# Pairs of experts' tiles in an attention and mixture-of-experts kernel: earlier gathers and transposes, another order on VectorE, other buffers

## The chip, the cores and the metric

The kernel runs on one core of one Trainium2 chip. The metric is the device time of one execution in microseconds (us); lower is better. Five engines share the work: TensorE (PE in the profile, its weight loads PEld), VectorE (DVE), ScalarE (ACT), GpSimd (POOL) and SyncE (SP), which here only issues DMAs.

## What is computed

The input is 2 x 2048 tokens of 512 features. It is normalized to xn. One branch is attention with a single head of 512 over xn, causal, with a residual; the other a mixture of eight experts, of which each token takes two. The result is x + s * silu(ffn).

```python
xn = _layernorm(x)
s = attention(xn)            # layernorm again, q, k, v, causal softmax, o_proj, + xn
scores = xf @ gate_w.T + gate_b + bias
top_scores, top_idx = top_k(scores, 2)
gates = softmax(top_scores)
comb = sum(one_hot(top_idx, 8) * gates[..., None], axis=1)
h = silu(einsum('td,ehd->teh', xf, w1) + b1)       # 512 -> 352, for each expert
y = einsum('teh,edh->ted', h, w2) + b2             # 352 -> 512
ffn = einsum('ted,te->td', y, comb)
return x + s * silu(ffn)
```

## The kernel before

Everything is f32. The whole program stands in one order written out by hand (`manual_schedule`): each engine and each DMA queue takes its instructions in the order of the Python code, and a late one holds all behind it on the same engine.

**Projections and routing.** Tokens come in 8 blocks of 512. For each block the rows are normalized, transposed and multiplied by folded weights to q and v; the results go to memory in HBM. Blocks 0 to 4 use a scheme of seven half-size products instead of eight (`seven_products`, L395), whose additions VectorE makes into tiles `so` of a ring of four (L403), stored from ScalarE's queue. A normalized row also goes, as its two 16-bit halves, to `zu_d`, from which the experts' rows are gathered later. `route` (L455) is a generator: each `yield n` lets the loop at its call emit n projection units (each 8 matmul instructions) before it goes on. It picks two experts per token, counts, gives each (token, expert) a slot, and inverts that by one-hot matmuls (`inv_p`) into `toki`, the token of each slot. Then it gathers the first `FIRST` tiles of rows, and from `half` and `first` finds the expert of every half tile (`eidi`) and its bias column (`b1sel`, L674 to L702).

**Experts.** There are 68 tiles of 128 slots. Tiles 6 to 57 in the order of work are 26 pairs of one expert each (`paired`); six single tiles go ahead of them and ten after. A tile i passes through these steps, each a function:

- `gather(i)` (L799): GpSimd fetches its rows `xs` from `zu_d` by an indirect DMA;
- `turn(i)` (L868): SP transposes the 16-bit halves by DMA to `xhT`; `join(i)` (L873): VectorE puts the halves together to `xT`;
- `up(i)` (L907) on TensorE, or `up_pair(i)` (L952) with seven products for two tiles; the pairs take weight differences `w1s` made by `w1_sums` (L927) and row sums made by `x_sums` (L940), and VectorE adds the products to `h` (L975);
- `turn_h(i)` (L992): ScalarE scales h, GpSimd splits it to `hu` (L996), SP transposes it to `huT`; `join_h(i)` (L1003): VectorE joins it, ScalarE applies SiLU;
- `down(i)` (L1016) on TensorE, three tiles behind; `keep_y(i)` (L1031): the result goes through `y` to `y_d`.

`experts_step(i)` (L1038) orders this for a single tile, `pair_step(i)` (L1063) for a pair. Steps -5 to -1 (L1212) only fill the pipeline between the last projection units. Steps 0 to 5 are single tiles; after steps 1 to 4 `w1_sums` makes the four differences of two experts each, the third of each four on GpSimd (L938).

**Memory.** Buffers come from pools on a stack at either end of SBUF. A pool opened with `reuse_waits="tile"` waits tile by tile for what lay there before; the others wait for the whole of each earlier pool that they overlap. The pool `xtp`, with the tiles `xhT` and `xT`, is opened after routing's pools `rp` and `hot` are closed and lies where they lay. `wsp`, with `w1s`, is opened once the projections' pools are closed.

**Attention** follows, in steps of one or two tiles of queries, with seven products where it can (`values_first`, `values_next`, `values_end`, `combine_p`). `gate(s)` takes two gathered rows of y for each token to the gate, and the last pair's output is made ahead (`make_ahead`).

Of the kernel before, what the change touches and what calls it, by code (L numbers as in the profile page):

```python
# [13 lines left out]
U16 = mybir.dt.uint16  # L14
# [12 lines left out]
def gated_attention_moe(  # L27
# [166 lines left out]
    def load_w1(e):  # L194
        if e == 0:

            w1p = wp.enter_context(tc.tile_pool(name="w1p", bufs=1, reuse_waits="tile"))
            w1.append(w1p.tile([P, E, ND, H], F32, name="w1"))
        nc.sync.dma_start(
            out=w1[0][:, e, :, :], in_=w1_t[e].rearrange("(c p) h -> p c h", p=P)  # L200
        )
# [193 lines left out]
    def seven_products(b, of_q):  # L395
# [7 lines left out]
        outs = [fp.tile([P, 2, D], F32, name=f"so_{tag}_{i}", tag="so", bufs=4) for i in range(2)]  # L403
# [51 lines left out]
    def route():  # L455

        with ExitStack() as rt:
# [170 lines left out]
            for k, oh in enumerate((oh1, oh2)):  # L628
# [11 lines left out]
                for t0 in range(0, NT, GROUP):  # L640
# [19 lines left out]
                    yield 1  # L660
# [13 lines left out]
            GS = [P, E, NJ]  # L674
            ge = rp.tile(GS, F32, name="ge")
            begun = []
            for k in range(3):
                nc.vector.tensor_tensor(
                    ge, half.unsqueeze(1).to_broadcast(GS), first[:, k].to_broadcast(GS), ALU.is_ge
                )  # L680
                n = rp.tile([P, NJ], F32, name=f"begun{k}")
                over_e(n, ge, ALU.add)
# [7 lines left out]
            for e in range(E):  # L690
                nc.vector.tensor_scalar(ge[:, e, :], eid, float(e), None, ALU.is_equal)
            for c in range(NH):
                for e in range(E):
                    if e == 0:
                        nc.vector.tensor_scalar(
                            b1sel[:, c, :], ge[:, e, :], b1s[:, c, e : e + 1], None, ALU.mult
                        )
                    else:
                        nc.vector.scalar_tensor_tensor(
                            b1sel[:, c, :], ge[:, e, :], b1s[:, c, e : e + 1], b1sel[:, c, :],  # L700
                            ALU.mult, ALU.add,
                        )  # L702
# [52 lines left out]
    fold_st.close()  # L755
    both(0)
# [38 lines left out]
    xsp = st.enter_context(tc.tile_pool(name="xsp", bufs=6))  # L795
    xss = {}
    FIRST = 5
# [57 lines left out]
    xtp = st.enter_context(tc.tile_pool(name="xtp", bufs=1))  # L855
    hp = st.enter_context(tc.tile_pool(name="hp", bufs=3))
    yp = st.enter_context(tc.tile_pool(name="yp", bufs=3))
# [10 lines left out]
    def turn(i):  # L868
        xh = xtp.tile([P, 2 * ND, P], U16, name=f"xhT_{i}", tag="xhT", bufs=3)
# [3 lines left out]
    def join(i):  # L873
        xT = xtp.tile([P, ND, P], F32, name=f"xT_{i}", tag="xT", bufs=4)
# [52 lines left out]
    def w1_sums(e, parts):  # L927
# [6 lines left out]
        t = [w1s[0][:, e : e + 2, i] for i in range(4)]  # L934
        for i, x1, x2 in (1, b12, b11), (2, b22, t[0]), (3, b22, b12), (4, b21, t[1]):
            if i in parts:
                engine = nc.gpsimd if i == 3 else nc.vector
                engine.tensor_tensor(t[i - 1], x1, x2, ALU.subtract)  # L938
# [13 lines left out]
    def up_pair(i, meanwhile):  # L952
# [3 lines left out]
        hs = [hp.tile([P, H], F32, name=f"h_{i + k}", tag="h", bufs=4) for k in range(2)]  # L956
# [21 lines left out]
        meanwhile()  # L978
# [3 lines left out]
        add(c21, made(s3, t(3)), c12)  # L982
        p5 = made(s1, t(1))
# [8 lines left out]
    def turn_h(i):  # L992
        h = phs[i] if i in paired else hp.tile([P, H], F32, name=f"h_{i}", tag="h", bufs=4)
# [43 lines left out]

    def experts_step(i):  # L1038
# [8 lines left out]
        at(keep_y, -DOWN - 1)  # L1047
        if i >= 0:
            at(gather, FIRST)
        at(turn, 3)  # L1050
        if i + 1 not in xts:
            at(join, 1)
        if i < FULL:
# [9 lines left out]
    def pair_step(i):  # L1063
# [3 lines left out]
        turn(i + 3)  # L1067
        turn(i + 4)
        up_pair(i, lambda: join_h(i - 2))
        turn_h(i)  # L1070
        gather(i + FIRST + 1)
        turn_h(i + 1)
# [4 lines left out]
        for k in range(i + 2, i + 4):  # L1077
            join(k)
        if i + 2 in paired:
            x_sums(i + 2)  # L1080

# [134 lines left out]
    stage_a.close()  # L1216
    sm = right(att, name="sm2", bufs=4)
# [11 lines left out]
    for i in range(NS):  # L1229
# [17 lines left out]
        if i < paired.start:  # L1247
            if 0 < i <= E // 2:
                w1_sums(2 * (i - 1), (1, 2, 3, 4))
# [311 lines left out]
    for s in range(NT + OUT + 2):  # L1561
# [103 lines left out]
        elif fast and s == NT - 1:  # L1665
# [4 lines left out]
                + [lambda: combine_p(s - 1), lambda: gate(s - 1)],  # L1670
# [62 lines left out]
```

## Time and profile before

| | us |
|---|---|
| median of 3 runs (1054.21 to 1056.05) | 1054.82 |
| the profiled execution, in all | 1049.76 |
| its span, first to last instruction | 1048.1 |

| stage | from, us | to, us |
|---|---|---|
| projections and routing | 0 | 262.4 |
| six single tiles of the experts | 262.4 | 291.8 |
| 26 pairs | 291.8 | 540.4 |
| ten single tiles | 540.4 | 592.0 |
| attention | 592.0 | 1048.1 |

The stages are read off TensorE's timeline. The page groups instructions by source line, engine, operation and tiles; a row gives count, busy time, mean duration, and the idle time of the engine just before them with what ended it. The costliest rows of the parts concerned:

```profile
L996 POOL COPY hu<-h 128x704 uint16<-128x704 uint16 x68 | 63.7, 937 | 175.1 <-issue 129.6
...
L875 DVE COPY xT<-xhT 128x1024 uint16<-128x1024 uint16 x68 | 61.8, 916 | 25.2 <-DMA xhT<-xs 25.0
...
L975 DVE TENSOR_TENSOR h<-p,h 128x176 f32<-128x176 f32 x182 | 56.1, 337 | 15.2 <-PE p L968 8.0
L1005 DVE COPY ht<-huT 128x768 uint16<-128x768 uint16 x68 | 40.3, 592 | 33.2 <-DMA huT<-hu 31.4
```

### The profile page before, as it was taken

What the parts mean: (1) busy time and instruction counts of PE and PEld (TensorE: products, weight loads), DVE (VectorE), ACT (ScalarE), POOL (GpSimd) and SP (SyncE); (2) the same over time, 40 slices, a digit from 0 to 9 for tenths busy, and PEclk for the clock granted to TensorE, in tenths of its full rate; (3) what the DMA queues carried; (4) which work ended last, traced back from release to release, by engine and by line L of the source; (5) the groups of instructions that cost most, each with busy time, mean ns of one, the idle gap of its engine ahead of it and who ended that gap; (6) DMA issues with size and microseconds to landing.
All of it is one profiled execution on the core that took longest, in us unless ns stands there. A gap on an engine that the chain in (4) does not pass through costs nothing.

```text
span 1048.1 us, 13294 instructions
## 1 busy us (share of the span) xinstructions
PE 1027.8 (98%) x3836; PEld 643.9 (61%) x3836; DVE 735.2 (70%) x1449; ACT 367.2 (35%) x741; POOL 461.7 (44%) x474
## 2 busy tenths in 40 slices
PE   9998999999899999999999999999999999999997
PEld 5686887444466666677654346776764544447576
DVE  5796884796787767777754558786556556788667
ACT  3212122121244444444445423222334553542341
POOL 3363141002654434434433317444656777764272
PEclk9998999999999999999999999999999999999999
DMA  8699989964799999999999857535767868754361
GB/s 303 183 266 281 251 257 317 354 209 125 171 197 218 201 223 197 203 226 208 199 229 244 198 191 173 134 90 133 191 172 235 257 185 224 196 143 116 95 158 41
DMA packets 300519, 209.41 MB, mean 200 GB/s; under 512 B 234520, under 2 KB 247576, under 8 KB 299424
## 3 DMA queue, kind: packets, MB, share of 16 engines
q1 hardware_dynamic: 280960, 145.60, 59.1%
q0 software_dynamic: 10560, 35.17, 13.0%
q10 hardware_dynamic: 8928, 27.79, 7.4%
q8 instruction: 33, 0.54, 0.2%
q14 instruction: 38, 0.31, 0.1%
HBM read 92.89 MB, written 60.03 MB: 146 GB/s over the span
## 4 chain that ended last, share of the span: by engine, by line
PE 73%; issue 8%; POOL 7%; DMA 7%; DVE 4%; SPq 1%; ACT 0%; POOLq 0%; DVEq 0%
PE ps L1122 13%; PE py L1025 9%; PE p L1174 8%; PE p L1382 8%; PE p L412 8%; PE po L1334 7%; PE p L968 7%; PE pj L353 3%; PE pw L219 3%; PE pj L358 3%; PE p L1334 2%; POOL xs L801 2%; DMA huT<-hu 2%; POOL hu L996 1%; DMA zuT<-zu 1%
## 5 line engine op out<-in xcount | busy, mean ns | idle before, releaser
L1025 PE MATMUL py<-w,ht 128*128 (+3 forms) x408 | 182.2, 593 | 0.0
L1122 PE MATMUL ps<-k,q 128*128 128x512 f32 (+3 forms) x416 | 143.0, 495 | 0.8 <-DMA q<-qt_d 0.8
L996 POOL COPY hu<-h 128x704 uint16<-128x704 uint16 x68 | 63.7, 937 | 175.1 <-issue 129.6
L1294 POOL COPY pu<-pT 128x1024 uint16<-128x1024 uint16 (+2 forms) x74 | 82.3, 1143 | 117.9 <-ACT pT L1284 58.1
L1025 PEld LDWEIGHTS py<-w,ht 128*128 128x128 f32 (+3 forms) x408 | 73.4, 184 | 83.6 <-issue 76.4
L1122 PEld LDWEIGHTS ps<-k,q 128*128 128x128 f32 x416 | 74.7, 190 | 68.4 <-issue 59.5
L801 POOL DMA_INDIRECT xs<-zu_d,toki x68 | 75.1, 1105 | 69.5 <-DVE toki L669 57.8
L1011 ACT ACTIVATE ht<-ht,b1sel 128x128 f32<-128x128 f32 (+3 forms) x228 | 71.1, 378 | 79.8 <-DVE ht L1005 79.5
L1479 POOL DMA_INDIRECT yg<-y_d,posi x64 | 68.3, 1067 | 38.1 <-DVE yg L1490 22.6
L1334 PE MATMUL po<-v,pT 128*128 128x512 f32 x182 | 81.1, 592 | 0.0
L875 DVE COPY xT<-xhT 128x1024 uint16<-128x1024 uint16 x68 | 61.8, 916 | 25.2 <-DMA xhT<-xs 25.0
L276 POOL COPY zu<-z 128x1024 uint16<-128x1024 uint16 x32 | 35.2, 1100 | 83.2 <-DVE z L261 83.2
L975 DVE TENSOR_TENSOR h<-p,h 128x176 f32<-128x176 f32 x182 | 56.1, 337 | 15.2 <-PE p L968 8.0
L1005 DVE COPY ht<-huT 128x768 uint16<-128x768 uint16 x68 | 40.3, 592 | 33.2 <-DMA huT<-hu 31.4
L1316 DVE COPY pT<-puT 128x1024 uint16<-128x1024 uint16 (+2 forms) x74 | 55.3, 777 | 9.6 <-DMA puT<-pu 9.5
L425 DVE TENSOR_TENSOR so<-p,so 128x512 f32<-128x512 f32 x70 | 46.0, 685 | 18.3 <-DMA v_d<-so 8.2
L1334 PEld LDWEIGHTS po<-v,pT 128*128 128x128 f32 x182 | 34.2, 190 | 38.1 <-issue 36.4
L1284 ACT ACTIVATE pT<-pT,nm 128x1024 f32<-128x1024 f32 x14 | 16.1, 1148 | 111.4 <-DVE nm L1210 72.3
L1500 DVE SCALAR_TENSOR_TENSOR o<-xo,xscale,o 128x512 f32<-128x512 f32 x30 | 28.8, 967 | 33.2 <-ACT o L1497 31.0
L1180 DVE TENSOR_TENSOR pT<-p,pT 128x512 f32<-128x512 f32 x49 | 32.9, 687 | 25.9 <-PE p L1174 18.7
L1284 ACT ACTIVATE pT<-ps,nm 128x512 f32<-128x512 f32 (+3 forms) x52 | 30.0, 581 | 59.4 <-DVE nm L1210 38.9
L1508 POOL TENSOR_TENSOR o<-o,yg 128x512 f32<-128x512 f32 x30 | 41.4, 1381 | 14.9 <-DVE o L1500 14.7
(276 smaller groups left out, 2046.1 us busy)
## 6 DMA issues: line engine op xcount, KB each, us to landing
y_d<-y SPq DMA_DIRECT2D x68, 256.0 KB
zu_d<-zu SPq DMA_DIRECT2D x32, 264.0 KB
kt_d<-kT ACTq DMA_DIRECT2D x8, 1024.0 KB
k<-kt_d SPq DMA_DIRECT2D x32, 256.0 KB
q<-qt_d SPq DMA_DIRECT2D x32, 256.0 KB
v<-v_d SPq DMA_DIRECT2D x32, 256.0 KB
xo<-in_x_dram SPq DMA_DIRECT2D x32, 256.0 KB
x<-in_x_dram SPq DMA_DIRECT2D x30, 256.0 KB
```

The lines of the kernel that those rows point to most:

```text
L412: nc.tensor.matmul(ps[:, r, :], lhsT=lhs[:, c, ts(r, P)], rhs=rhs[:, c, :], start=(c == 0), stop=(c == 1),)
L801: nc.gpsimd.indirect_dma_start(out=xs, out_offset=None, in_=zu_d, in_offset=bass.IndirectOffsetOnAxis(ap=toki[:, order[i] : order[i] + 1], ...
L968: nc.tensor.matmul(ps, lhsT=x[:, c], rhs=y(c).rearrange("p o h -> p (o h)"), start=(c == 0), stop=(c == ND // 2 - 1),)
L996: nc.gpsimd.tensor_copy(hu[:, :, :H], h.bitcast(U16).rearrange("p (d h) -> p h d", h=2))
L1011: nc.scalar.activation(ht[:hn, c, at], ht[:hn, c, at], AF.Silu, bias=b1sel[:hn, c, j : j + 1])
L1025: nc.tensor.matmul(py[at, :], lhsT=ht[:k, c, at], rhs=rhs[n], start=(c == 0), stop=(c == NH - 1),)
L1122: nc.tensor.matmul(ps[:, :w], lhsT=aqs[seq[s] // 2][:, c, ts(t % 2, P)], rhs=aks[first + j][:, c, :w], start=(c == 0), stop=(c == ND - 1),)
L1174: nc.tensor.matmul(ps, lhsT=x[:, c], rhs=y[:, c], start=(c == 0), stop=(c == ND // 2 - 1))
L1294: nc.gpsimd.tensor_copy(pu[:, : 2 * w].rearrange("p (h d) -> p h d", h=2), turned[s][:, k : k + w].bitcast(U16).rearrange("p (d h) -> p h ...
L1334: nc.tensor.matmul(dst, lhsT=turned[s][:, ts(k, P)], rhs=avs[first + k // BT][:, k % BT, cols], start=(start and k == k0), stop=(k == k1 - 1),
L1382: nc.tensor.matmul(dst, lhsT=a[:, k], rhs=v(k), start=(k == 0), stop=(stop and k == n - 1))
L1479: nc.gpsimd.indirect_dma_start(out=y, out_offset=None, in_=y_d, in_offset=bass.IndirectOffsetOnAxis(ap=posi[k][:, n : n + 1], axis=0),)
```

## The change

1. `route`: the yield before the last group's inversion is left out. The comparisons are laid out with experts innermost, summed by `sum_e`; the eight comparisons and 24 scalings for `b1sel` become one comparison and three multiplications with a reduction.
2. A pool `xhp` with four `xhT` tiles is opened beside `xsp`, before `route`; `xsp` has seven tiles, `FIRST` is 6, and `turn` runs four tiles ahead instead of three.
3. `w1_sums(e, i)` makes one difference; three are made in each of steps 0 to 5 until all 16 are done, ahead of `join_h` and `up`; one of them is on GpSimd.
4. `pair_step`: the joins come first; `join_h(i - 2)` (`meanwhile`) comes after three additions; both `turn_h` come before the second gather.
5. `y` has two buffers instead of three, from a pool opened after the projections' pools are closed; `h` has three instead of four. `keep_y` of tiles 0 and 1 is on ScalarE.
6. The `so` tiles of v of blocks 0 to 3 have a pool `sop` of four tiles of their own.
7. Near the end of attention, `gate` comes between the first two and the last two operations of `combine_p`.

```diff
     def load_w1(e):
         if e == 0:
-
+            half_st.close()
...
-        outs = [fp.tile([P, 2, D], F32, name=f"so_{tag}_{i}", tag="so", bufs=4) for i in range(2)]
+        pool = fp if of_q or b == SEVEN - 1 else sop
+        outs = [pool.tile([P, 2, D], F32, name=f"so_{tag}_{i}", tag="so", bufs=4) for i in range(2)]
...
-                    yield 1
+                    if k == 0 or t0 + GROUP < NT:
+                        yield 1
                     invert()
...
-            GS = [P, E, NJ]
+            GS = [P, NJ, E]
             ge = rp.tile(GS, F32, name="ge")
+
+            def sum_e(dst):
+                nc.vector.tensor_reduce(dst, ge, AX.X, ALU.add)
+
             begun = []
             for k in range(3):
                 nc.vector.tensor_tensor(
-                    ge, half.unsqueeze(1).to_broadcast(GS), first[:, k].to_broadcast(GS), ALU.is_ge
+                    ge, half.unsqueeze(2).to_broadcast(GS),
+                    first[:, k, :, 0].unsqueeze(1).to_broadcast(GS), ALU.is_ge,
                 )
                 n = rp.tile([P, NJ], F32, name=f"begun{k}")
-                over_e(n, ge, ALU.add)
+                sum_e(n)
...
-            for e in range(E):
-                nc.vector.tensor_scalar(ge[:, e, :], eid, float(e), None, ALU.is_equal)
+            nc.vector.tensor_scalar(eid, eid, -1.0, float(E), ALU.mult, ALU.add)
+            mine_e = rp.tile(GS, F32, name="mine_e")
+            nc.vector.tensor_tensor(
+                mine_e, eid.unsqueeze(2).to_broadcast(GS),
+                rank[:, :, 0].unsqueeze(1).to_broadcast(GS), ALU.is_equal,
+            )
             for c in range(NH):
-                for e in range(E):
...
+                nc.vector.tensor_tensor(
+                    ge, mine_e, b1s[:, c, :].unsqueeze(1).to_broadcast(GS), ALU.mult
+                )
+                sum_e(b1sel[:, c, :])
...
+    half_st = ExitStack()
+    sop = half_st.enter_context(tc.tile_pool(name="sop", bufs=4, reuse_waits="tile"))
...
-    xsp = st.enter_context(tc.tile_pool(name="xsp", bufs=6))
+    xsp = st.enter_context(tc.tile_pool(name="xsp", bufs=7))
+    xhp = st.enter_context(tc.tile_pool(name="xhp", bufs=4))
     xss = {}
-    FIRST = 5
+    FIRST = 6
...
-    yp = st.enter_context(tc.tile_pool(name="yp", bufs=3))
...
     def turn(i):
-        xh = xtp.tile([P, 2 * ND, P], U16, name=f"xhT_{i}", tag="xhT", bufs=3)
+        xh = xhp.tile([P, 2 * ND, P], U16, name=f"xhT_{i}", tag="xhT")
...
-        for i, x1, x2 in (1, b12, b11), (2, b22, t[0]), (3, b22, b12), (4, b21, t[1]):
-            if i in parts:
-                engine = nc.gpsimd if i == 3 else nc.vector
-                engine.tensor_tensor(t[i - 1], x1, x2, ALU.subtract)
+        x1, x2 = ((b12, b11), (b22, t[0]), (b22, b12), (b21, t[1]))[i]
+        engine = nc.gpsimd if (e, i) == (0, 2) else nc.vector
+        engine.tensor_tensor(t[i], x1, x2, ALU.subtract)
...
-        hs = [hp.tile([P, H], F32, name=f"h_{i + k}", tag="h", bufs=4) for k in range(2)]
+        hs = [hp.tile([P, H], F32, name=f"h_{i + k}", tag="h") for k in range(2)]
...
         nc.scalar.copy(c11, made(a11, b(0, 0)))
-        meanwhile()
         p2 = made(a12, b(1, 0))
         add(c12, made(s2, t(2)), c11)
         add(c11, p2, c11)
         add(c21, made(s3, t(3)), c12)
+        meanwhile()
         p5 = made(s1, t(1))
...
+    sums_left = [(e, k) for e in range(0, E, 2) for k in range(4)]
...
-        at(keep_y, -DOWN - 1)
+        if 0 <= i - DOWN - 1 < NS:
+            keep_y(i - DOWN - 1, *[nc.scalar.copy] * (i < paired.start))
         if i >= 0:
             at(gather, FIRST)
-        at(turn, 3)
+        at(turn, 4)
         if i + 1 not in xts:
             at(join, 1)
+        for _ in range(3 if 0 <= i < paired.start else 0):
+            if sums_left:
+                w1_sums(*sums_left.pop(0))
...
         gather(i + FIRST)
-        turn(i + 3)
-        turn(i + 4)
+        for k in range(2):
+            turn(i + 4 + k)
+        for k in range(2):
+            join(i + 2 + k)
         up_pair(i, lambda: join_h(i - 2))
-        turn_h(i)
+        for k in range(2):
+            turn_h(i + k)
         gather(i + FIRST + 1)
-        turn_h(i + 1)
         join_h(i - 1)
         down(i - DOWN)
         keep_y(i - DOWN, nc.scalar.copy)
         down(i - DOWN + 1)
-        for k in range(i + 2, i + 4):
-            join(k)
...
     stage_a.close()
+    yp = st.enter_context(tc.tile_pool(name="yp", bufs=2))
...
-            if 0 < i <= E // 2:
-                w1_sums(2 * (i - 1), (1, 2, 3, 4))
...
-                + [lambda: combine_p(s - 1), lambda: gate(s - 1)],
+                + [lambda: combine_p(s - 1, (1, 3)), lambda: gate(s - 1)]
+                + [lambda: combine_p(s - 1, (2, 4))],
```

## The prediction

> **What bounds the kernel now.** I read the page first, then busy time by stretch, then TensorE's timeline where a stretch shows idle time, then who ended those waits.
>
> The page, row of busy time:
>
> ```profile
> PE 1027.8 (98%) x3836; PEld 643.9 (61%) x3836; DVE 735.2 (70%) x1449; ACT 367.2 (35%) x741; POOL 461.7 (44%) x474
> ```
>
> TensorE sets the time, and only its gaps can be won. "Busy" hides part of them (an instruction's modelled end runs into the gap), so I count from start to start. Busy time by stretch (us, PE, PEld, DVE, ACT, POOL, clock, DMA, GB/s):
>
> ```profile
> 262.40:293.10 30.70, 25.91 (x75) 14.31 (x74) 23.41 (x27) 8.11 (x19) 20.29 (x17) 0.94 0.77 170
> ...
> 340.10:446.60 106.50, 104.31 (x441) 70.97 (x440) 76.95 (x168) 48.34 (x121) 44.10 (x45) 1.00 1.07 206
> 446.60:540.40 93.80, 93.60 (x401) 64.51 (x400) 69.02 (x149) 44.48 (x110) 41.42 (x41) 1.00 1.04 215
> ```
>
> The start of the experts (six single tiles, before the pairs) is the worst stretch, and the only one of these whose clock is below 1.00. TensorE there:
>
> ```profile
> 262.01 0.59 PE L358 MATMUL pj<-wvo,kT 128*128 128x512 f32 x1
> 264.67 11.40 PE L915 MATMUL ph<-w,xT 128*128 x32 [2.06 <-issue]
> ...
> 280.49 2.63 PE L915 MATMUL ph<-w,xT 128*128 x8 [1.85 <-DVE xT L875]
> ...
> 294.21 0.83 PE L968 MATMUL p<-w1s,xs 128*128 x4 [0.96 <-DVE xs L949]
> ```
>
> and all engines around the first gap:
>
> ```profile
> 256.47 2.30 DVE L699 SCALAR_TENSOR_TENSOR b1sel<-ge,b1s,b1sel 128x76 f32<-128x76 f32 x7
> ...
> 258.99 6.77 SPq L870 DMA_TRANSPOSE xhT<-xs  x4
> ...
> 263.77 1.37 DVE L875 COPY xT<-xhT 128x1024 uint16<-128x1024 uint16 x2 [5.00 <-DMA xhT<-xs]
> ```
>
> The rows were gathered from 243.08 on, but SP issues the first transposes only when routing's last sum ends (258.77): their tile lies in routing's freed buffers. The later gaps follow GpSimd; the chain of waits:
>
> ```profile
> 288.89 2.30 POOL w1s L938
> ...
> 294.72 4.58 DMA huT<-hu
> ```
>
> The chain has such a subtraction in each of four steps. Each stands ahead of the next copy `hu`, hence of the transpose `huT`, `join_h`, and behind it, in VectorE's order, the next tiles' work. In the pairs VectorE's order matters; TensorE, then VectorE, in one bad step:
>
> ```profile
> 389.30 0.86 PE L968 MATMUL p<-w1s,xs 128*128 x4 [0.51 <-DVE xs L949]
> ...
> 392.51 0.86 PE L968 MATMUL p<-w1s,xT 128*128 x4 [0.56 <-DVE h L975]
> ```
> ```profile
> 385.35 0.89 DVE L1005 COPY ht<-huT 128x768 uint16<-128x768 uint16 x1 [2.54 <-DMA huT<-hu]
> ...
> 391.65 0.56 DVE L1005 COPY ht<-huT 128x768 uint16<-128x768 uint16 x1 [1.95 <-DMA huT<-hu]
> ```
>
> A late `huT` holds VectorE, and behind it the two joins and the sums `xs` that TensorE's third product needs, then the additions that free PSUM.
>
> [...] Here 98% busy goes with the gaps above. [...] the clock of the first stretch is 0.94, a loss of 0.06 x 30.7 = 1.8 us; but one gap of 2.06 us came before it, and the 1.85 us gap at 280.49 was not followed by slow matmuls. [...] Here one xT copy took 0.69 us at 265.90 and 2.15 us at 278.28 beside GpSimd's subtraction.
>
> **The change part by part.** The sum is made against the profiled execution (span 1048.1, 1049.8 in all); the runs' median of 1054.8 lies 5.0 above that, which I carry over unchanged.
>
> *Start, TensorE's own work.* An up takes 2.36 us and a down 2.58 (540.45 to 542.81 to 545.39, unhindered). Up to the first pair it has 6 ups and 3 downs: 14.2 + 7.7 = 21.9. The last projection ends issuing at 262.01 + 0.43 = 262.44. An undisturbed pair step takes 9.33 (312.11 to 321.44), the second starts at 302.43, so the first one's effective start is 293.10. 30.7 - 21.9 = 8.8 us are lost, 1.8 of them to the clock.
>
> *Start, what the edits leave.* The last inversion no longer waits behind a projection unit: its operands were ready at 237.33 and it ran at 241.32 after a unit of 3.43, so token indices and all six gathers come about 3.5 sooner. The last sums: three comparisons of 0.79 and three strided reductions of 1.18 now reduce along the innermost axis; VectorE's 1024-wide reduction at 1.21 gives about 0.75 for 608, my estimate. Then 8 x 0.12 + 3 x 0.25 + 21 x 0.33 = 8.6 become one compare and three times multiply and reduce, 0.8 + 3 x 1.55 = 5.4, plus 0.2 for one more scalar operation. They end near 250.8 instead of 258.8. The transpose tile now has a home that routing doesn't use, so SP starts it when gathers land (4.4 us), near 245, and xT0 and xT1 are joined before 255. That clears TensorE's first gap, except for a PSUM bank that ScalarE may still be reading (its copy ends at 263.23): 0.5 us left. The half clock should go with it.
>
> The 16 weight subtractions: three a step, in steps 0 to 5, now ahead of `join_h` and `up`, one alone on GpSimd. VectorE then runs 15 x 0.9 = 13.5, six or seven joins x 0.7 = 4.9, four join_h x 0.56 = 2.2, x_sums 1.7: 22.3 us. It cannot begin the subtractions before 262.6 (their tile overlays the projections' operands), so it ends near 285, while TensorE, freed, wants the first pair at 262.9 + 21.9 = 284.8. They run side by side with next to no slack; hu0 at 266.8, huT0 4.2 later and join_h near 272 put the first down some 0.5 late, and I allow 0.5 more. If the subtractions' tile also waited for the last projections' stores (near 266.5), the stage would lose 3.9 more; by the sizes of the tiles it doesn't reach them, so I take 0. Left: 1.5 of 8.8, gain 7.3 (3.4 to 8.3).
>
> *Pairs.* From 302.43 to 540.45 lie 25 steps: 238.0 - 25 x 9.33 = 4.7 lost. Now each transpose is issued a tile sooner, with a fourth buffer; the two joins (1.4 to 1.9) stand at the head of the step, where their transposes are a whole step old; `join_h(i-2)` comes after three additions, not before all seven. So sums `xs` follow `join_h(i-1)` directly, 1.4 us sooner, against shortages of 0.3 to 0.8, and the bank that the seventh product needs is freed ahead of `join_h`. VectorE has 7 x 0.34 + 2 x 0.92 + 2 x 0.59 + 2.07 = 7.5 of 9.33 us. The second gather now follows both `hu` copies, 1.2 us sooner for `huT`, later for a row that has a step to spare. I leave 1.0 lost: gain 3.7 (0 to 4.7).
>
> *Rings.* y falls from 3 to 2, h from 4 to 3. h: the copy that frees the slot ran a step before, nothing. y: stores are issued up to 3.5 us after the copy (309.73 to 313.24), landing took 4.93 in the chain (565.95), and the slot is wanted 9.33 after the copy: 0.9 us to spare. Queued behind a late ScalarE copy are the pair's first eviction and `join_h`'s SiLUs. Not below nothing, since a smaller ring speeds nothing; up to 0.5 x 26 = 13 against; I take 0.
>
> *sop.* Values' outputs leave the shared ring. At 86.38 VectorE waits 3.3 for a store, but then waits 2.6 more for the last `zuT`, which releases TensorE at 92.27; the transposes are held by full DMA queues. I take 0 (-0.5 to +3).
>
> *End.* Gating now fills VectorE while the last two sums wait; it stood 0.8 us for ScalarE at 1027.88, and the bank that TensorE misses at 1033.78 (gap 1.67) is freed behind that. Gain 0.8 (0 to 0.9). Copying y of two tiles on ScalarE: under 1.4 us of VectorE, within the start's margin.
>
> Sum: 7.3 + 3.7 + 0 + 0 + 0.8 = 11.8. Profiled span about 1036.3; median 1054.8 - 11.8 = **1043.0**.
>
> **Rivals.** *B, pairs' stalls stay*: DMA share 1.07 says that the transposes are late because DMA is full; against it, 446.6 to 540.4 lost 0.2 us of idle at 1.04. Gain 7.3 + 0.8: 1046.7. *C, VectorE bounds the start*: 22.3 us in 22 leaves nothing for GpSimd's interference (0.69 to 2.15 for one copy); 4 us back, and a part of the pairs': gain 4.5, 1050.3. *D, the y ring (slower)*: if stores land more than 0.9 us later than 4.93 in every pair, at 0.5 a step 13 us are lost and 11.8 won: 1056.0; it outweighs the gain from 0.45 us a step. For it: DMA is full; against: only the worst delays reach the bound. *E, nothing*: the gaps are refilled by others, 1054.8.
>
> **How the numbers follow.** A 0.60, B 0.18, C 0.10, D 0.08, E 0.04. A's own range is 1040 to 1046; with B and the near part of C the range is 1039.5 to 1049.5. Faster by over 0.2% (2.1 us, about what can be told from no change): A, B, C = 0.88; same 0.04; slower 0.08.
>
> **What would show it.** SP's first transposes near 245 and no gap before `up`; no half-clock stretch near 265; GpSimd with one `w1s`; first pair near 285; pair steps of 9.33 without the waits on `xs` and `h`; a gap of some 0.9 near the end. Wrong if ScalarE's y copies wait for DMA, if VectorE has no idle time from 263 to 285 and TensorE waits on it, or if the pairs' losses remain.

## The result, and the profile after

| | before | changed |
|---|---|---|
| median, us | 1054.51 (1050.91 to 1056.05, 4 runs) | 1039.58 (1037.34 to 1043.04, 4 runs) |
| profiled execution, in all | 1049.76 | 1043.04 |
| its span | 1048.1 | 1041.3 |

The ratio of the changed kernel to the one before is 0.9866, 95% interval 0.9828 to 0.9905: faster. The predicted 1043.0 is 3.4 us above the measured median. The medians lie 14.9 us apart, the two profiles only 6.7: the kernel before was profiled 4.8 us below its median, the changed one in the slowest of its four runs.

The ratios here and below use each kernel's runs within 1.5% of its fastest, which cuts off the upper part of the wide spread of the kernel before (1042.4 to 1086.5 in 59 runs of one series); a median set beside a median differs from the ratio for that reason, and both are given where they disagree.

The page, row of busy time:

```profile
PE 1023.0 (98%) x3836; PEld 643.8 (62%) x3836; DVE 727.0 (70%) x1426; ACT 366.7 (35%) x743; POOL 463.4 (45%) x471
```

Busy time by stretch (us, PE, PEld, DVE, ACT, POOL, clock, DMA, GB/s): the six single tiles up to the effective start of the first pair, then pairs.

```profile
259.28:292.16 32.88, 26.45 (x91) 15.87 (x89) 24.46 (x30) 10.28 (x24) 19.33 (x16) 0.99 0.88 171
300.00:530.00 230.00, 230.00 (x993) 159.86 (x992) 165.37 (x368) 106.58 (x270) 101.98 (x97) 1.00 1.01 213
```

In the pairs TensorE is busy all of the time. The start has not become shorter: 32.9 us against 30.7. TensorE there:

```profile
259.28 7.26 PE L923 MATMUL ph<-w,xT 128*128 x24
268.36 2.63 PE L923 MATMUL ph<-w,xT 128*128 x8 [1.82 <-DVE xT L883]
271.67 2.84 PE L1032 MATMUL py<-w,ht 128*128 x6 [0.68 <-ACT ht L1018]
...
286.63 0.83 PE L975 MATMUL p<-w1s,xs 128*128 x4 [1.03 <-DVE xs L956]
...
293.24 1.54 PE L975 MATMUL p<-w1s,xT 128*128 x4 [3.98 <-DVE h L982]
294.57 4.08 PE L1032 MATMUL py<-w,ht 128*128 x5
```

The gap before `up` is gone: 259.28 is the last projection's start, 258.85, plus its 0.43. But there are new ones, above all 3.98 us within the first pair, and behind it five products take 4.08 us, some 0.82 each instead of 0.43: the half clock. The granted clock was 0.50 from 291.3 to 298.1, and 1.00 ahead of that from 258.9 to 290. The timelines of SP, VectorE and GpSimd say what was late:

```profile
240.29 17.71 SPq L878 DMA_TRANSPOSE xhT<-xs  x5
...
261.82 3.48 DVE L945 TENSOR_TENSOR w1s<-w,w1s 128x704 f32<-128x704 f32 x1
...
262.16 1.68 POOL L945 TENSOR_TENSOR w1s<-w 128x704 f32<-128x704 f32 x1
...
272.71 3.98 POOL L1003 COPY hu<-h 128x704 uint16<-128x704 uint16 x1 [4.15 <-ACT h L1001]
...
284.86 2.21 SPq L878 DMA_TRANSPOSE xhT<-xs  x1
...
292.24 0.69 DVE L883 COPY xT<-xhT 128x1024 uint16<-128x1024 uint16 x1 [4.23 <-DMA xhT<-xs]
```

A subtraction that takes 0.89 alone took 3.48 while GpSimd had its own and a `hu`, and the `xT` behind it came late (268.36). A `hu` that takes 0.77 took 3.98 beside VectorE's run of subtractions. The chain goes on: later `hu`, later `huT`, and behind it on SP the transpose of tile 9, issued at 284.86. The first pair's second join (292.24) waits for it, with that pair's additions behind it. From the issue to that join 7.4 us pass, so part of the gap is a slow transfer and not the chain: the DMA share was 1.16 from 284 to 293.

In the pairs, who ended VectorE's waits between 302 and 530 us (total, times, longest), before and after:

```profile
DVE ht L1005 <- DMA huT<-hu: 22.9, 21, 2.5
DVE xT L875 <- DMA xhT<-xs: 19.1, 16, 2.9
```
```profile
DVE h L982 <- PE p L975: 55.4, 25, 3.8
DVE xT L883 <- DMA xhT<-xs: 4.3, 11, 1.3
```

VectorE now waits for TensorE, 2.2 us a step, and hardly for a transpose. The page's rows that answer to those of before:

```profile
L1003 POOL COPY hu<-h 128x704 uint16<-128x704 uint16 x68 | 65.6, 982 | 170.3 <-issue 125.5
...
L982 DVE TENSOR_TENSOR h<-p,h 128x176 f32<-128x176 f32 x182 | 55.5, 337 | 59.0 <-PE p L975 55.4
...
L883 DVE COPY xT<-xhT 128x1024 uint16<-128x1024 uint16 x68 | 45.6, 690 | 12.7 <-DMA xhT<-xs 12.5
```

`xT` fell from 916 to 690 ns. In the pairs of before, copies of `xT` beside a `hu` took up to 1.26 us, most of the others 0.69; in the pairs of the changed kernel none runs beside a `hu`, and none takes more than 0.70. Elsewhere, TensorE's largest gap of the projections before and after, and the one near the end:

```profile
92.27 1.94 PE L319 MATMUL pg<-zT,gw 128*32 128x512 f32 x8 [4.07 <-DVE zT L302]
```
```profile
91.02 1.07 PE L319 MATMUL pg<-zT,gw 128*32 128x512 f32 x8 [2.41 <-DVE zT L302]
...
1027.03 2.00 PE L1347 MATMUL p<-v,pT 128*128 128x256 f32 x8 [1.36 <-DVE o L1412]
```

The table splits the profiles as the prediction did, from start to start: the end of the last projection; what the start loses ahead of the first pair (its start, less the end of the projections, less 21.9) and in it (its step less 9.33); what the other pairs lose (last pair's start, less the second's, less 24 x 9.33); VectorE's waits for `huT` from 310 to 530. All in us; the experiments' rows are for what follows.

| kernel | span | projections end | lost ahead of first pair | in it | other pairs | waits for `huT` | median |
|---|---|---|---|---|---|---|---|
| before | 1048.1 | 262.4 | 7.5 | 1.3 | 4.3 | 22.2 | 1054.5 |
| changed | 1041.3 | 259.3 | 3.1 | 7.9 | 0.1 | 0 | 1039.6 |
| e1, changed again | 1037.2 | 258.5 | 3.1 | 3.3 | 0.1 | 1.2 | 1041.1 |
| e2, changed without `sop` | 1044.2 | 262.3 | 3.1 | 6.3 | 0.1 | 0 | 1043.6 |
| e3, before with `sop` | 1064.9 | 259.8 | 5.2 | 1.3 | 23.8 | 40.8 | 1055.6 |
| e4, changed, first joins late | 1039.1 | 261.4 | 3.1 | 2.0 | 0.1 | 0 | 1039.3 |
| e5, changed, old order in pairs | 1062.8 | 261.1 | 3.1 | 1.6 | 20.8 | 56.0 | 1057.9 |
| e6, changed, old subtractions | 1039.8 | 261.8 | 3.5 | 1.4 | 0.1 | 0 | 1037.3 |
| e7, before with the early home | 1053.5 | 257.8 | 4.2 | 0.9 | 18.2 | 34.8 | 1052.6 |
| e8, before, `join_h` later | 1047.3 | 261.9 | 8.2 | 0.9 | 2.1 | 10.8 | 1049.3 |
| e9, changed, joins last | 1037.8 | 261.9 | 3.1 | 1.5 | 0.1 | 0 | 1037.3 |
| e10, changed, `join_h` early | 1036.5 | 258.0 | 3.1 | 4.4 | 0.1 | 0 | 1042.1 |
| e11, before with smaller rings | 1051.5 | 261.6 | 8.1 | 1.3 | 7.4 | 30.5 | 1057.5 |
| e12, changed, subtractions behind `up` | 1033.5 | 258.4 | 0.9 | 1.6 | 0.1 | 0 | 1035.4 |

Between the two profiles: projections 3.2, start -2.2, pairs 4.2, and 1.6 behind the last pair's start (0.5 in its own step, 0.8 in the ten single tiles, the rest in attention): 6.8, or 6.7 before rounding.

### The profile page after: what moved, and what is told of

Read it like the earlier page. It is cut to its first block, busy times and chain, and to the rows that moved or that the text cites. A ratio compares the mean times of both kernels' runs of the same rounds, so it can differ in the third digit from the quotient of the medians.

```text
span 1041.3 us, 13227 instructions
## 1 busy us (share of the span) xinstructions
PE 1023.0 (98%) x3836; PEld 643.8 (62%) x3836; DVE 727.0 (70%) x1426; ACT 366.7 (35%) x743; POOL 463.4 (45%) x471
## 4 chain that ended last, share of the span: by engine, by line
PE 77%; DMA 11%; DVE 4%; POOL 3%; SPq 2%; issue 2%; ACT 1%; ACTq 0%; POOLq 0%; DVEq 0%
PE py L1032 16%; PE ps L1136 13%; PE p L975 10%; PE p L1188 8%; PE p L1395 8%; PE po L1347 8%; PE p L413 3%; PE pj L353 3%; PE pj L358 3%; DMA zuT<-zu 3%; PE ph L923 2%; DMA w<-in_w_t_dram 2%; PE p L1347 2%; DVE w1s L945 1%; PE pw L219 1%
## 5 line engine op out<-in xcount | busy, mean ns | idle before, releaser
L810 POOL DMA_INDIRECT xs<-zu_d,toki x68 | 79.9, 1175 | 69.7 <-DVE toki L671 54.7
L1297 ACT ACTIVATE pT<-pT,nm 128x1024 f32<-128x1024 f32 x14 | 16.1, 1148 | 112.5 <-DVE nm L1224 73.2
L1040 ACT COPY y<-py 128x512 f32<-128x512 f32 x54 | 31.5, 584 | 65.2 <-PE py L1032 48.7
L883 DVE COPY xT<-xhT 128x1024 uint16<-128x1024 uint16 x68 | 45.6, 690 | 12.7 <-DMA xhT<-xs 12.5
L1194 DVE TENSOR_TENSOR pT<-p,pT 128x512 f32<-128x512 f32 x49 | 32.9, 687 | 25.9 <-PE p L1188 22.2
```

The source lines that it names most:

```text
L810: nc.gpsimd.indirect_dma_start(out=xs, out_offset=None, in_=zu_d, in_offset=bass.IndirectOffsetOnAxis(ap=toki[:, order[i] : order[i] + 1], ...
```

## The experiments

Four series. The median of the kernel before was 1058.57 in that of e1 to e4, 1053.98 for e5 to e8, 1051.09 for e9 to e12, so a run is compared by its ratio, or with runs of its own series.

**e1: the changed kernel again.** No edit.

> The changed kernel once more, for what recurs between executions. Theory: TensorE's gap of 4.0 us in the first pair (its seventh product waiting for VectorE, which waits for the transpose of tile 9) is a matter of order and recurs at 3 to 5 us; the half clock of 6.8 us behind it [...] may be missing (then the span is 2 to 3.4 us shorter). Rival: the gap is chance too and is under 1 us here. The 25 pair steps are 9.33 us each under both.

1041.1 us (1037.92 to 1044.37, 6 runs), ratio 0.9846 (0.9786 to 0.9906). In its first pair TensorE waited 1.64 instead of 3.98 us at the same instruction, and no half clock followed (1.00 on average from 258 to 305):

```profile
290.29 0.86 PE L975 MATMUL p<-w1s,xT 128*128 x4 [1.64 <-DVE h L982]
290.99 5.32 PE L1032 MATMUL py<-w,ht 128*128 x12
```

The transpose of tile 9 was issued as soon after the pair's first product as before (0.7 us, against 0.6), but joined 5.1 us later instead of 7.4: the difference between the two gaps is the transfer. The other pairs again lose nothing. What a profile shows in the first pair is one draw (3.3 or 7.9 lost); the rhythm of the other pairs was the same in both.

**e2 and e3: `sop` taken out, and `sop` alone.** e2 undoes part 6 of the change in the changed kernel, e3 adds it to the kernel before.

```diff
-            half_st.close()
...
-        pool = fp if of_q or b == SEVEN - 1 else sop
-        outs = [pool.tile([P, 2, D], F32, name=f"so_{tag}_{i}", tag="so", bufs=4) for i in range(2)]
+        outs = [fp.tile([P, 2, D], F32, name=f"so_{tag}_{i}", tag="so", bufs=4) for i in range(2)]
```

> The changed kernel without the four extra tiles for v's outputs. Theory (DMA sets the gap near 88 us, as the prediction had it): gap 2 to 4.5 us as in both kernels, median within 2 us of the changed kernel's; the half clock at 91 us, 3.4 us, may come or go. Rival (the extra tiles shortened it): the gap is 4 us again with the half clock behind it, median 3 to 5 us above the changed kernel's.

1043.6 us (1038.44 to 1046.15, 6 runs), ratio 0.9857 (0.9796 to 0.9919).

> The kernel before with the four extra tiles for v's outputs alone. Theory (DMA sets the gap): no change beyond 2 us. Rival (extra tiles matter): projections end near 259 us instead of 262.4, 3 to 5 us faster.

1055.56 us (1046.81 to 1066.58, 22 runs), ratio 1.0036 (1.0003 to 1.0069); its profiled execution was its longest. In the profile of e2 the large gap and half the clock behind it are back (0.89 on average from 80 to 110 us, as before, against 1.00 in the changed kernel):

```profile
92.57 1.93 PE L318 MATMUL pg<-zT,gw 128*32 128x512 f32 x8 [4.22 <-DVE zT L301]
94.44 3.52 PE L411 MATMUL p<-kT,wqk 128*128 128x256 f32 x8
```

Over all profiles, start to start, this gap lost 0.95 to 4.38 us in the five kernels without `sop` and 1.29 to 2.95 in the nine with it, and another near 171 us opened in six of those with it (1.1 to 2.7), in none without. The projections end at 261.2 on average without and 260.0 with it. In the ratios neither run shows a gain: e2's interval holds e1's ratio, and e3's ratio is not below 1. By the medians of all runs `sop` would be worth 2.5 us (e2 against e1) and 3.0 us (e3 against the kernel before), which is within the scatter of the runs: a gain is not shown, and a small one is not excluded. Most of the 3.2 us between the two first profiles is their draw, since the two averages lie only 1.2 apart.

**e4: the first pair's joins late.** For the first pair alone the two joins go behind `join_h(i - 1)`.

```diff
-        for k in range(2):
+        for k in range(2 if i > paired.start else 0):
             join(i + 2 + k)
...
         join_h(i - 1)
+        for k in range(2 if i == paired.start else 0):
+            join(i + 2 + k)
```

> The changed kernel, with the two joins of the first pair step alone put back behind join_h(i - 1). Theory (the joins at the head wait for tile 9's transpose and hold the additions that free the seventh product's bank): the 4.0 us gap goes, the first pair step falls from 17 to 9.5-11 us, and the median is 4 us lower, up to 7 where the half clock followed the gap. Rival (VectorE is simply full there): a gap of 3 us or more returns at the next pair's third product, and the time stays.

1039.33 us (1035.02 to 1043.48, 6 runs), ratio 0.9825 (0.976 to 0.989). The seventh product's wait is gone; a wait for `xs` stays:

```profile
289.47 0.83 PE L975 MATMUL p<-w1s,xs 128*128 x4 [1.72 <-DVE xs L956]
...
291.93 0.76 PE L975 MATMUL p<-w1s,xT 128*128 x4
```

The first pair loses 2.0 us. So the gap came from the join that stood ahead of the additions and waited for its transpose. Against e1 the median is 1.8 us lower, with intervals that overlap: the gap's cause is shown, a gain in the time is not.

**e6: the old subtractions in the changed kernel.** Four in each of steps 1 to 4 behind the step, the third of each four on GpSimd.

```diff
-        engine = nc.gpsimd if (e, i) == (0, 2) else nc.vector
+        engine = nc.gpsimd if i == 2 else nc.vector
...
-        for _ in range(3 if 0 <= i < paired.start else 0):
-            if sums_left:
-                w1_sums(*sums_left.pop(0))
...
+            for k in range(4 if 0 < i <= E // 2 else 0):
+                w1_sums(2 * (i - 1), k)
```

> The changed kernel with the weight subtractions where they were: four after each of steps 1 to 4, the third of each on GpSimd. Theory (moving them onto VectorE ahead of join_h won nothing, since VectorE is then full and holds GpSimd): the start loses 4 to 7 us of TensorE, no more than the 6.4 and 11.4 us of the changed kernel's two profiles; median within 3 us of it or lower. Rival (the prediction's step: GpSimd's subtractions were in the way): three gaps of 2.0, 0.6 and 0.6 us return and the start loses 3 us more than the changed kernel.

1037.33 us (1036.2 to 1041.46, 6 runs), ratio 0.9845 (0.9804 to 0.9886). The start loses 4.9 us, less than in any profile of the changed kernel (6.4 and 11.0): moving the subtractions bought nothing. GpSimd's and VectorE's own, in the timelines:

```profile
273.08 2.29 POOL L945 TENSOR_TENSOR w1s<-w 128x704 f32<-128x704 f32 x1
...
273.77 2.15 DVE L883 COPY xT<-xhT 128x1024 uint16<-128x1024 uint16 x1
```

Each `xT` beside a GpSimd subtraction takes 2.15 instead of 0.69, in three of the four steps. That is the old loss, and it is no larger than the one that the change put in its place. The longest `hu` from 255 to 292 took 0.96 us, against 3.98 in the changed kernel beside VectorE's subtractions.

**e7: the early home alone.** The kernel before, with the `xhT` tiles in a pool of three opened beside `xsp`, ahead of `route`.

```diff
     xsp = st.enter_context(tc.tile_pool(name="xsp", bufs=6))
+    xhp = st.enter_context(tc.tile_pool(name="xhp", bufs=3))
...
-        xh = xtp.tile([P, 2 * ND, P], U16, name=f"xhT_{i}", tag="xhT", bufs=3)
+        xh = xhp.tile([P, 2 * ND, P], U16, name=f"xhT_{i}", tag="xhT")
```

> The kernel before with the transposes' tiles alone moved beside xs, ahead of routing. Theory: SP's first transposes start while routing's last sums run, TensorE's gap of 2.06 us before the first up and the half clock behind it go; 2 to 4 us at that place, the later gaps of 2.0, 0.6 and 0.6 us and the pairs' stalls stay. Rival: the gap moves on to the next tiles' joins and the first pair starts no sooner after the projections than 30.7 us.

1052.58 us (1041.29 to 1071.32, 22 runs), ratio 0.9972 (0.9943 to 1.0002). SP and TensorE:

```profile
242.35 13.77 SPq L871 DMA_TRANSPOSE xhT<-xs  x4
```
```profile
257.83 9.63 PE L916 MATMUL ph<-w,xT 128*128 x32
```

The first gap is gone with this edit alone, and the start loses 5.1 instead of 8.8 us: 3.7 gained. The ratio's 0.28% would be 3 us, though its interval just reaches 1. The rest of the start's edits is not needed to close this gap.

**e12: the subtractions behind `up`.** The changed kernel with all 16 on VectorE, still three a step, but behind `join_h` and `up` in the order; and e4's edit.

```diff
-        engine = nc.gpsimd if (e, i) == (0, 2) else nc.vector
-        engine.tensor_tensor(t[i], x1, x2, ALU.subtract)
+        nc.vector.tensor_tensor(t[i], x1, x2, ALU.subtract)
...
-        for _ in range(3 if 0 <= i < paired.start else 0):
-            if sums_left:
-                w1_sums(*sums_left.pop(0))
         if i < FULL:
             at(join_h, -2)
         at(up, 0)
         at(copy_w1, 1)
         at(turn_h, 0)
+        for _ in range(3 if 0 <= i < paired.start else 0):
+            if sums_left:
+                w1_sums(*sums_left.pop(0))
```

> The changed kernel with the weight subtractions all on VectorE, three a step as in the change, but behind join_h and up instead of ahead of them; and the first pair's two joins behind join_h(i-1). Theory (the start loses by what stands behind the subtractions in VectorE's order, and by GpSimd's one subtraction running against VectorE): start loses 2 to 5 us instead of 6 to 11, no gap of 2 us near 266, no half clock near 294; median 1033 to 1037. Rival (the gaps go to other places, VectorE's 22 us of work fill the stage anyhow): start loses 6 to 9, median 1038 to 1041.

1035.42 us (1030.45 to 1038.53, 6 runs), ratio 0.9865 (0.9816 to 0.9913). TensorE up to the first pair and in it:

```profile
266.20 2.63 PE L923 MATMUL ph<-w,xT 128*128 x8 [0.59 <-DVE xT L883]
...
281.14 1.36 PE L974 MATMUL p<-w,xT 128*128 x8
283.88 0.84 PE L974 MATMUL p<-w1s,xs 128*128 x4 [1.38 <-issue]
```

The start loses 2.5 us, the least of all, with no half clock (1.00 from 258 to 305). VectorE does all 16 subtractions and is busy 16.6 of the 18 us from 263 to 281, so the work fits when it stands behind what the step waits for. The run changes two things ahead of the first pair, the place and the engine of one subtraction, and does not tell their shares. It has the lowest median of all runs, 1.9 below e9 in its series, but its ratio is that of the changed kernel: better than the kernel before, not shown to be better than the change.

**e5: the old order in the pairs.** The changed kernel with the joins last, `join_h(i - 2)` ahead of the seven additions and the second gather between the two `turn_h`; the transposes stay sooner.

```diff
-        for k in range(2):
-            join(i + 2 + k)
         up_pair(i, lambda: join_h(i - 2))
-        for k in range(2):
-            turn_h(i + k)
+        turn_h(i)
         gather(i + FIRST + 1)
+        turn_h(i + 1)
...
         down(i - DOWN + 1)
+        for k in range(i + 2, i + 4):
+            join(k)
...
         nc.scalar.copy(c11, made(a11, b(0, 0)))
+        meanwhile()
...
-        meanwhile()
```

> The changed kernel with VectorE's order of before in the pair step (join_h(i - 2) after the first product, the joins at the step's end, the second gather between the hu copies); transposes stay a tile sooner. Theory (VectorE's order kept the pairs from their 9.33 us): TensorE loses 3 to 15 us over the 25 steps, 1.5 to 2 us in single steps, and the median is 4 to 12 us above the changed kernel's with a wider spread. Rival (the sooner transposes did it): all 25 steps stay at 9.33 us, median within 2 us.

1057.89 us (1051.37 to 1064.55, 22 runs), ratio 1.0063 (1.0034 to 1.0092): the whole gain is gone. The profiled execution was its longest, so the losses seen in it lie at the upper end. VectorE's waits (310 to 530), then TensorE in one bad step:

```profile
DVE ht L1012 <- DMA huT<-hu: 56.0, 30, 4.6
```
```profile
443.27 0.76 PE L975 MATMUL p<-w,xs 128*128 x4
447.25 1.11 PE L975 MATMUL p<-w1s,xT 128*128 x4 [3.21 <-DVE h L982]
```

VectorE stood 4.60 us at `huT` ahead of the additions that free the seventh product's bank. So the change lives by the new order in the pairs, and sooner transposes of rows don't replace it.

**e8: `join_h(i - 2)` later, in the kernel before.**

```diff
         nc.scalar.copy(c11, made(a11, b(0, 0)))
-        meanwhile()
...
         add(c21, made(s3, t(3)), c12)
+        meanwhile()
```

> The kernel before with join_h(i - 2) alone put after three additions. Theory (the order of VectorE's work matters): the waits of TensorE's seventh product for h go, those of the third product for xs stay; the 25 steps lose a third to two thirds of what the kernel before loses in the same rounds. Rival (transposes matter): they lose as much as before, 4 us or more.

1049.32 us (1040.48 to 1058.15, 22 runs), ratio 0.9997 (0.9969 to 1.0025). VectorE's waits for `huT` are halved and this profile's pairs lose 2.1 us instead of 4.3. By the ratio the time gains at most 0.3%; by the medians of all runs it is 4.7 us lower than the kernel before. So the move alone may carry a part of the gain, and not the whole.

**e9 and e10: one move of the pairs' order undone at a time.** e9 puts the joins last again, as in e5's diff; e10 puts `join_h(i - 2)` ahead of the additions again, as in e5's diff. The rest of the change stays.

> The changed kernel with one of the three moves in the pairs undone: the two joins of rows stand again at the end of the step, right ahead of the row sums; join_h(i-2) stays behind three additions and the second gather behind both copies hu. Theory (both moves are needed, since a late transpose of either kind can hold VectorE at its own place): the waits that remain end on VectorE's xs, before the third product; pairs lose 3 to 8 us in the profile, median 1043 to 1049. Rival 1 (the joins' place alone matters): as with the whole old order, 1053 to 1060. Rival 2 (only join_h's place matters): no loss in the pairs, median 1037 to 1042.

1037.31 us (1032.81 to 1039.51, 6 runs), ratio 0.9875 (0.9828 to 0.9922). No loss in the pairs behind the first and no wait of TensorE for VectorE there: the theory written for this run fell, and its time and its pairs are as its rival 2 had them. With `join_h` later, the joins' place doesn't matter behind the first pair. In 26 joins of the pairs `xT` takes 1.26 us beside `hu` again, and that costs nothing.

> The changed kernel with another of the three moves undone: join_h(i-2) stands again ahead of all seven additions; the joins stay at the head of the step. Theory: the waits that come back end on VectorE's h, before the seventh product, as most did with the whole old order; pairs lose 5 to 15 us, median 1046 to 1055. Rival 1 (only the joins' place matters): no loss in the pairs, median 1037 to 1042. Rival 2 (the gather's place, which stays changed here, is what matters): also 1037 to 1042, told from the former by the run with the joins last.

1042.06 us (1036.51 to 1045.52, 17 runs), ratio 0.9929 (0.9903 to 0.9955). The theory fell here too: the profiled execution, one of its fastest, loses nothing behind the first pair and shows no wait of the kind that was expected there. The median is 4.8 us above e9's, but e9 differs in the first pair as well: like e4 it has no join at the head of that pair, and loses 1.5 us in it. e10 keeps the changed kernel's joins there and loses 4.4, at the same instruction as the changed kernel:

```profile
290.82 0.86 PE L975 MATMUL p<-w1s,xT 128*128 x4 [2.75 <-DVE h L982]
```

Every run has its mean granted clock on record. The three of e10 at 1.000 took 1036.5 to 1038.2 us, the four at 0.995 took 1043.5 to 1045.3; 0.005 of 1044 us is 5.2 us, so by this estimate most of what the slower runs lose goes with the clock, in a stage that is not seen. In the pairs VectorE now waits for ScalarE, and hardly for a transpose:

```profile
DVE h L982 <- ACT ht L1018: 39.9, 23, 1.8
...
DVE xT L883 <- DMA xhT<-xs: 0.6, 1, 0.6
```

Neither run brings back e5's loss; it takes two of the moves undone together, or the third, the gather's place, which only e5 undid in the changed kernel. The table speaks for the latter: in the six kernels with the gather between the two copies `hu`, VectorE waits 10.8 to 56.0 us for `huT`; in the eight with both copies first, 0 or 1.2. GpSimd in a bad step of before, and in a step after:

```profile
394.96 1.20 POOL L996 COPY hu<-h 128x704 uint16<-128x704 uint16 x1 [7.87 <-issue]
396.33 1.24 POOL L801 DMA_INDIRECT xs<-zu_d,toki  x1 [0.16 <-ACT ht L1011]
397.57 0.77 POOL L996 COPY hu<-h 128x704 uint16<-128x704 uint16 x1
```
```profile
437.34 1.88 POOL L1003 COPY hu<-h 128x704 uint16<-128x704 uint16 x2 [4.69 <-issue]
439.36 1.31 POOL L810 DMA_INDIRECT xs<-zu_d,toki  x1
```

The gather puts 1.4 us between the copies and its packets ahead of the second `huT`. The move alone was not tried, so this is a reading of the traces and not shown.

**e11: the smaller rings alone.** The kernel before with `y` of two and `h` of three.

```diff
-    yp = st.enter_context(tc.tile_pool(name="yp", bufs=3))
+    yp = st.enter_context(tc.tile_pool(name="yp", bufs=2))
...
-        hs = [hp.tile([P, H], F32, name=f"h_{i + k}", tag="h", bufs=4) for k in range(2)]
+        hs = [hp.tile([P, H], F32, name=f"h_{i + k}", tag="h", bufs=3) for k in range(2)]
...
-        h = phs[i] if i in paired else hp.tile([P, H], F32, name=f"h_{i}", tag="h", bufs=4)
+        h = phs[i] if i in paired else hp.tile([P, H], F32, name=f"h_{i}", tag="h", bufs=3)
```

> The kernel before with the smaller rings alone: y two buffers instead of three (from the same pool), h three instead of four. Prediction's step and theory: nothing, ratio 0.997 to 1.003, and no ScalarE copy of y waits for a DMA. Rival D: stores land too late in the pairs' steps, ScalarE's y copies wait for a DMA, and pairs lose more: ratio 1.005 or above. That would also explain why the changed kernel with the old order in the pairs came out slower than the kernel before.

1057.48 us (1041.89 to 1066.44, 14 runs), ratio 1.0024 (0.997 to 1.0078). All that ScalarE's copies of y wait for in the pairs:

```profile
ACT y L1033 <- PE py L1025: 34.5, 21, 1.9
ACT y L1033 <- ACT ht L1011: 4.8, 7, 0.7
```

No DMA among them: rival D's mechanism isn't there. The time is less clear. The ratio leaves room for 0.8% of loss, and by the medians of all runs (1057.48 against 1051.09) this kernel is 6.4 us slower; in its profile VectorE waits 30.5 us for `huT` instead of 22.2. So a cost of the smaller rings under the old order is not excluded, and it would fit e5, which has both and is slower than the kernel before. Under the new order the pairs behind the first lose nothing with the same rings.

## Why the prediction was right

Faster was right, and the size nearly so, but by two errors that cancel: the start brought next to nothing of its 7.3 us, and the pairs some three times their 3.7. That the sum came close is luck, and the median lies at the lower edge of the range of 1039.5 to 1049.5.

- **First gap: right, and more.** Transposes near 245 came at 240.29, routing's last sums ended at 249.0 instead of 250.8, a reduction of 608 took 0.79 against the estimated 0.75. TensorE's `up` follows the projections with no gap, where 0.5 was left for it. e7 shows that the tiles' home brings this by itself: 3.7 us.
- **The start as a whole: the step that failed.** Predicted was a gain of 7.3, with 1.5 us left. In the two profiles of the changed kernel 11.0 and 6.4 us are left of 8.8. It failed in two terms. "They run side by side with next to no slack" allowed about 1 us; ahead of the first pair 3.1 us were lost, the same in each of seven profiles with these subtractions, while instructions of VectorE and GpSimd took longer side by side than alone, both ways (0.89 to 3.48 on VectorE, 0.77 to 3.98 on GpSimd). That the two engines held each other is my inference from these durations. I took for each subtraction its duration alone (0.9), though I had named that risk in rival C. e12 shows what place and engine cost together: 0.9 lost with the same subtractions behind `up`, all on VectorE. The second term is the pairs' own: the joins at the head of the step, "where their transposes are a whole step old". For the first pair they are not even one short single-tile step old: with a late `huT` ahead of it on SP, the transpose of tile 9 was issued 0.6 and 0.7 us after the pair's first product and joined 7.4 and 5.1 us later. 7.9 and 3.3 us were lost in that pair, 2.0 with the joins late (e4).
- **Half clock: went and came back.** Before, the granted clock was 0.50 from 265.2 to 268.7, behind the gap of 2.06 us; in the changed kernel it was 1.00 there, but 0.50 from 291.3 on, within the new gap of 3.98 that ends at 293.24, and until 298.1. At the same instruction e1's gap of 1.64 and e10's of 2.75 had none (1.00 on average from 258 to 305 in both). What decides it was not shown: the last section has a gap of 2.06 with slow products behind it and one of 2.79 without.
- **Pairs: mechanism right, size too small.** 25 steps of exactly 9.33 with none of the waits, where 1.0 us was left as lost. Against the profile of before that is worth 4.2 us (0.5 more in the last step) for a predicted 3.7. But that profile was a lucky draw: other kernels with the whole old order (e3, e7, e11) lost 23.8, 18.2 and 7.4 in the pairs. The failing step is "which I carry over unchanged": the 5.0 us between profile and median held stalls of the same kind (an inference from those profiles), and they went too. Rival B, that they stay, is refuted. The later `join_h` alone (e8) does not carry the whole gain, and the changed kernel needs neither the joins' place (e9) nor the later `join_h` (e10) for its rhythm; what the gather's place does alone stays open.
- **Rings: mechanism right, size open.** No copy of y waits for a DMA in e11, and stores of the changed kernel land 4.4 us after issue at the median. A cost of 0 fits e11's ratio, but its median is 6.4 us higher; under the new order no loss is seen.
- **sop: not refuted.** Taken at 0, with a gain of up to 3 allowed; the profiles differ by 3.2 us, e2 and e3 show no gain in the ratios and 2.5 and 3.0 us in the medians. The gap moves about from run to run. That full DMA queues hold the transposes is the prediction's inference; the DMA share was 1.08 from 81.4 to 91.5, from the issue of the last `zuT` to the end of VectorE's wait for it.
- **End: small.** VectorE's wait for ScalarE is gone, and the gap fell from 1.67 to 1.36 where 0.9 was expected: 0.3 instead of 0.8. The sum that frees the bank stands behind gating in both kernels. From VectorE's first operation of `combine_p` to that sum it took 11.67 us before (1021.63 to 1033.30) and 10.79 now (1015.76 to 1026.55), but the first one began only 1.97 us ahead of TensorE's group of products (1017.73) instead of 2.54 (1024.17), which takes back 0.6 of the 0.9.
- **Rival C: half right.** It had the interference and a gain of the start that is mostly lost, but not for its reason, a VectorE that is full: VectorE was busy 18.1 of the 22 us from 263 to 285, and e12 gives it all 16 subtractions and loses least. And the pairs gave back nothing.

An estimate of the median's 14.9 from the profiles: pairs 9.9 to 13.3 (mean loss of before, e7 and e11, with the whole old order: 4.3, 18.2, 7.4, against 0.1; the higher figure with e3's 23.8, from its longest run), projections 1.2 (the two means of 261.2 and 260.0), the start about 0 (8.8 against 11.0, 6.4 and, in e2 with the same start, 9.4), behind the last pair's start 1.6: 12.7 to 16.1. The start, the largest term of the prediction, gave next to nothing, and the pairs some three times what was put down.

## What to carry to other kernels

Where an engine's order is written by hand, put an operation that waits for a DMA behind the work that the bounding engine needs next, and filler work behind the operations that a step waits for: the same instructions lost 20.8 us (in a long run) or 0.1 in the pairs by their place alone, and 3.1 or 0.9 ahead of them by their place and the engine of one of them. Look at the first step of a new order by itself, since what is a whole step old in the steady rhythm may just have been issued there. When a kernel's runs spread by several per cent and the profile is one draw, price a stall that is removed at the distance between profile and median as well.

## What was not expected of the hardware

The half clock does not go by the length of the gap alone. Near 88 us, with the same work, TensorE in e12 and in e6:

```profile
90.99 1.07 PE L319 MATMUL pg<-zT,gw 128*32 128x512 f32 x8 [2.79 <-DVE zT L302]
91.98 1.99 PE L413 MATMUL p<-kT,wqk 128*128 128x256 f32 x8
```
```profile
90.23 1.69 PE L319 MATMUL pg<-zT,gw 128*32 128x512 f32 x8 [2.06 <-DVE zT L302]
91.86 3.01 PE L413 MATMUL p<-kT,wqk 128*128 128x256 f32 x8
```

A gap of 2.79 us was followed by products at full speed (1.99 us for the second eight), one of 2.06 by slow ones (3.01); the mean clock from 80 to 110 us was 1.00 in e12 and 0.94 in e6.

The order in the pairs bears on the spread as well as the mean. The kernel before ran from 1042.4 to 1086.5 us in one series of 59 runs, and e5 from 1051.4 to 1064.6 in 22; e10 ran from 1036.5 to 1045.5 in 17, and the changed kernel's ten runs (4 and 6) lie between 1037.3 and 1044.4. In all eight profiles with both `hu` copies ahead of the gather, every step behind the first pair's takes 9.33 us. What spread is left goes in part with the granted clock, as in e10 (1036.5 to 1038.2 us at 1.000, 1043.5 to 1045.3 at 0.995).
